# A feed-forward half in four sweeps of one batch each, with streamed weights and operands that are never stored

## The chip, the core and the metric

The kernel runs on one core of a Trainium2 chip. The metric is the device time of one execution in microseconds, the median of several runs. The engines are named as in the profile: PE (TensorE, matmul and transposes), PEld (its weight load), DVE (VectorE), ACT (ScalarE), POOL (GpSimd) and SP (SyncE, which here issues nearly all DMAs, in order, on one queue).

## What is computed

The input is 4 batches of 1024 rows with 2048 columns. An adaptive layer norm feeds a long convolution along the columns (the first half, not touched by the change), whose gated result is added to x. Then a second adaptive layer norm feeds a linear layer, to which a sum of 16 low-rank updates is added, and its gated result is added to x. Cut to this:

```python
h = _layernorm(x, axis=-1) * (1 + ca) + sa
x = x + ga * _L0_attn_ref(h, ...)
h = _layernorm(x, axis=-1) * (1 + cb) + sb
x = x + gb * _L0_ffn_ref(h, W, bias, A, Bf, coeffs, scales)
...
def _L0_ffn_ref(x, W, bias, A, Bf, coeffs, scales):
    out = jnp.einsum('bsd,od->bso', x, W) + bias
    xa = jnp.einsum('bsd,erd->ebsr', x, A)
    upd = jnp.einsum('ebsr,eor,e->bso', xa, Bf, coeffs * scales)
    return out + upd
```

ga and gb, sa and sb, ca and cb come from a small product of the conditioning vectors with a modulation matrix. In f32 the second linear layer is a product of 4096 x 2048 by 2048 x 2048.

## The kernel before

**First half.** A modulation product, the making of the convolution's Toeplitz matrices, then 32 row blocks (r = 0 to 31, 128 rows each) go through the convolution on PE. In gaps of it, the low-rank updates are merged into the weights and the weights are split and written to DRAM as `wcd` (function `merge`). Each row block's result is written to DRAM as `x1d`, with its mean and scale kept in `ln2` (`conv_post`).

**Feed-forward half.** The product is done by a scheme of seven products in place of eight: rows and columns of the left operand and of the weights are split in halves, seven sums of quarters of the left operand are each multiplied by a sum of quarters of the weights (number i, 0 to 6), and the four quarters of the output are sums of the seven products. Every f32 operand is held as two f16 numbers, a high and a low part; a product is high times high, high times low and low times high. So one 128x512 accumulator of one product takes 8 x 3 = 24 matmuls of 128x128 by 512 columns.

- `wcd` holds the seven weight sums for each of two column quarters q (512 columns in each half of the output's columns): 7 sums of 2 MiB for each q.
- Two passes, q = 0 and q = 1. In each, the seven weight sums of this q stay in SBUF (14 tiles of 1 MiB), and 16 units u of 256 rows go through (`ffn_unit`, L815 to L880).
- Pass q = 0 makes the left operands (`left`, L759 to L805): two row blocks of `x1d` are loaded (L765), normalized on ACT (L766), transposed on PE in groups of four (L776) and scaled from PSUM to SBUF on ACT (L778). Then four sums on DVE and seven casts on ACT (L788) and subtractions on DVE (L789) make the seven f16 pairs. Each pair is used and also written to DRAM (`lfd`, L790). This work is given out in small steps between the products of the units ahead (`tick`, with the plan `LPLAN`).
- Pass q = 1 loads those pairs again (`left_load`, L809).
- A unit's seven products run in the order 0, 4, 5, 1, 6, 2, 3. Three PSUM accumulators, X, Y and Z, take them; where two products are added to each other the second is accumulated on the first in PSUM (0 and 1 in X, 4 and 2 in Y, while Z takes 5, 6 and 3 as a running sum). ACT copies partial results out (L834), DVE adds them, multiplies with the gate (L849), adds the residual with the bias (L850), and SP stores the 128x512 block (L851). The residual's four blocks are loaded at the start of a unit (L843) and the bias is added to them at once (L844).
- The gate and bias rows of a batch are loaded as broadcasts twice per batch, and the gate is scaled on DVE (L1198).

**Order.** The code gives the instructions in one order, which is their priority; a scheduler at compile time puts each engine's instructions into a fixed order from it, by what it reckons to be ready. On the chip, each engine and each queue takes its list in order. PSUM has five accumulators of one bank for products (`ACC = 5`) and two for transposes (`TPS = 2`).

**Where the halves meet.** The first unit's operands are made in steps during the last two row blocks of the convolution (r = 30 and 31, `LEFT0`). Weights of the first product are loaded into tiles of their own when the merges are done (`early`), those of the second and third into the row tiles x0 to x3 of the first half as these come free.

Of the kernel before, what the change touches and what calls it, by code (L numbers as in the profile page):

```python
# [12 lines left out]
F32 = mybir.dt.float32  # L13
# [16 lines left out]
NU = 16  # L30
# [5 lines left out]
class Net:  # L36
# [722 lines left out]
    def left(self, pl, u, res):  # L759
        nc, v = self.nc, self.nc.vector  # L760
        b = u // 4
        xs = []
        for r in range(2):
            x = pl["x2"].tile([P, D], F32, tag=f"x2{r}", name="x2")
            nc.sync.dma_start(out=x, in_=self.x1d[2 * u + r])  # L765
            nc.scalar.activation(  # L766
                x, x, AF.Identity, bias=self.ln2[:, 2 * u + r, 0:1], scale=self.ln2[:, 2 * u + r, 1:2]
            )
            xs.append(x)
        yield  # L770
        t = pl["t"].tile([P, NC, 2, P], F32, tag="t", name="gt")
        for c0 in range(0, NC, 2):
            tp = self.tps.tile([P, 2, 2, P], F32, tag="t", name="tp2")
            for c in range(2):
                for r in range(2):
                    nc.tensor.transpose(tp[:, c, r], xs[r][:, ds(P * (c0 + c), P)], self.ident)  # L776
            for c in range(2):
                nc.scalar.activation(  # L778
                    t[:, c0 + c], tp[:, c], AF.Identity,
                    bias=self.sb[:, c0 + c, b : b + 1], scale=self.cb[:, c0 + c, b : b + 1],  # L780
                )
            yield
        a11, a12 = t[:, 0:HC, 0, :], t[:, HC:NC, 0, :]
        a21, a22 = t[:, 0:HC, 1, :], t[:, HC:NC, 1, :]

        def put(i, s):
            hl = pl["l"].tile([P, HC, 2, P], F16, tag="l", name="lf")
            nc.scalar.copy(hl[:, :, 0, :], s)  # L788
            v.tensor_tensor(hl[:, :, 1, :], s, hl[:, :, 0, :], SUB)  # L789
            STQ(nc).dma_start(out=self.lfd[u, i], in_=hl)  # L790
            res[i] = hl

        put(0, a11)
        s = pl["s"].tile([P, HC, P], F32, tag="s", name="s")
        v.tensor_tensor(s, a21, a22, ADD)
        put(4, s)
        v.tensor_tensor(s, s, a11, SUB)
        put(5, s)
        put(1, a12)
        v.tensor_tensor(a21, a11, a21, SUB)  # L800
        put(6, a21)
        v.tensor_tensor(s, a12, s, SUB)
        put(2, s)
        put(3, a22)
        yield  # L805

    def left_load(self, pl, u, i):
        hl = pl["l"].tile([P, HC, 2, P], F16, tag="l", name="lf")
        self.nc.sync.dma_start(out=hl, in_=self.lfd[u, i])  # L809
        return hl  # L810

    def left_again(self, pl, u):
        return {i: self.left_load(pl, u, i) for i in ORDER}

    def ffn_unit(self, pl, u, q, lf, wc, tick):  # L815
        nc, v = self.nc, self.nc.vector
        ps = {}

        def prod(i, name):
            first = name not in ps  # L820
            if first:
                ps[name] = self.acc.tile([P, 512], F32, tag="a", name="f" + name)
            n = 0
            for k in range(HC):
                for x, y in ((0, 0), (0, 1), (1, 0)):
                    nc.tensor.matmul(  # L826
                        ps[name], lf[i][:, k, x, :], wc[i][k // 4][:, k % 4, y, :],
                        start=(first and n == 0), stop=(n == 3 * HC - 1), skip_group_check=True,
                    )
                    n += 1  # L830

        def copy(name, tag):
            t = pl["e"].tile([P, 512], F32, tag=tag, name=tag)
            nc.scalar.copy(t, ps[name])  # L834
            return t

        def at(x, r, h):
            return x[ds(P * r, P), ds(1024 * h + 512 * q, 512)]

        xs = {}  # L840
        for r, h in ((0, 0), (1, 1), (0, 1), (1, 0)):
            x = pl["o"].tile([P, 512], F32, tag="o", name="xo")
            nc.sync.dma_start(out=x, in_=at(self.x1d[2 * u : 2 * u + 2].rearrange("r p d -> (r p) d"), r, h))  # L843
            v.tensor_tensor(x, x, self.gbias[:, h], ADD)  # L844
            xs[r, h] = x

        def finish(r, h, cv, t):
            x = xs[r, h]
            v.tensor_tensor(t, cv, self.gbt[:, h], MUL)  # L849
            v.tensor_tensor(x, x, t, ADD)  # L850
            STQ(nc).dma_start(out=at(self.io["out"][ds(256 * u, 256), :], r, h), in_=x)  # L851


        prod(0, "X")
        p1 = copy("X", "p1")
        tick()
        prod(4, "Y")
        p5 = copy("Y", "p5")
        tick()
        prod(5, "Z")  # L860
        p6 = copy("Z", "p6")
        tick()
        prod(1, "X")
        finish(0, 0, ps["X"], pl["e"].tile([P, 512], F32, tag="p7", name="fin"))
        v.tensor_tensor(p6, p6, p1, ADD)
        tick()
        prod(6, "Z")
        p7 = copy("Z", "p7")
        v.tensor_tensor(p5, p5, p1, ADD)
        v.tensor_tensor(p7, p7, p5, ADD)  # L870
        finish(1, 1, p7, p7)
        tick()
        prod(2, "Y")
        v.tensor_tensor(p6, p6, ps["Y"], ADD)
        finish(0, 1, p6, p6)
        tick()
        prod(3, "Z")
        v.tensor_tensor(p1, p1, ps["Z"], ADD)
        finish(1, 0, p1, p1)
        tick()  # L880


ORDER = (0, 4, 5, 1, 6, 2, 3)
# [7 lines left out]
LPLAN = ("LL", "LL", "LL", "LL", "L", "0", "")  # L891
# [4 lines left out]
EARLY = 2  # L896
RAW = 4
# [14 lines left out]
def net(ctx: ExitStack, tc: tile.TileContext, io):  # L912
# [7 lines left out]
    k.lfd = k.dram.tile([NU, 7, P, HC, 2, P], F16, tag="lfd", name="lfd")  # L920
# [156 lines left out]
    pr, wc, lf = {}, {}, {}  # L1077

    XW = {ORDER[1]: (0, 1), ORDER[2]: (2, 3)}

    def load_w(q, i):

        wc[i] = []
        for j in range(2):
            if i in XW:
                w = pl["x"].tile([P, D], F32, tag=f"x{XW[i][j]}", name=f"w{i}").bitcast(F16)
            else:
                w = pr["w" if i == ORDER[0] else "v"].tile([P, 2 * D], F16, tag=f"w{i}{j}", name=f"w{i}")
            wv = w.rearrange("p (k y n) -> p k y n", k=4, y=2)
            nc.sync.dma_start(out=wv, in_=k.wcd[q, i][:, 4 * j : 4 * j + 4])  # L1090
            wc[i].append(wv)

    def early():
        right.close()
        for name, bufs in (("w", 1), ("l", 8), ("t", 1), ("s", 1), ("x2", 1)):
            pr[name] = pool(p2, "p2" + name, bufs, "right")
        load_w(0, ORDER[0])

    def next_left(u):
        if u >= NU:  # L1100
            return iter(())
        lf[u] = {}
        return k.left(pr, u, lf[u])
# [3 lines left out]
    def step():  # L1107
        if r < R0:

            calls[0] += 1  # L1110
            if r > EARLY and calls[0] % 2 == 0:
                with tc.issue_after(k.lasta.ins), tc.issue_after(k.lastv.ins):
                    next(fill)
        elif "w" not in pr and next(fill, 0) == 0:
            early()
# [23 lines left out]
    for r in range(EARLY, 32):  # L1139
# [4 lines left out]
        if r == 31:  # L1144
            load_w(0, ORDER[1])
        if r == LEFT0:
            while "w" not in pr:
                step()
            lgen = next_left(0)
# [25 lines left out]
    take(lgen, 10)  # L1175
    gens = [next_left(1)]
    take(gens[0], 1)
    left.close()

    for name in ("v", "o", "e", "g"):  # L1180
        pr[name] = pool(p2l, "p2" + name, 5 if name == "o" else 1)
    for q in range(2):
        for i in ORDER:
            if i not in wc or q == 1:
                load_w(q, i)
            if q == 1:
                lf.setdefault(0, {})[i] = k.left_load(pr, 0, i)
        for u in range(NU):
            b = u // 4
            if u % 4 == 0:  # L1190
                ts_ = []
                for i in range(2):
                    t = pr["g"].tile([P, 2, 512], F32, tag=f"gb{i}", name=f"gb{i}")
                    src = k.gbd[i][b].rearrange("(h n) -> h n", h=2)[:, ds(512 * q, 512)]
                    nc.sync.dma_start(out=t, in_=src.partition_broadcast(P))
                    ts_.append(t)
                k.gbt, k.gbias = ts_
                nc.vector.tensor_scalar(k.gbt, k.gbt, k.ginv[:, b : b + 1], None, MUL)  # L1198
            plan = iter(LPLAN)

            def tick():
                if q == 1:
                    return
                for a in next(plan):
                    if a == "0":
                        gens[0] = next_left(u + 2)
# [64 lines left out]
```

## Time and profile before

| | us |
|---|---|
| runs: median of 3 (lowest to highest) | 2134.47 (2133.88 to 2139.61) |
| the profiled execution's own time | 2133.88 |
| its span, first to last instruction | 2132.1 |
| mean granted TensorE clock | 0.988 |
| first product of the feed-forward half starts | 911.2 |
| its second pass starts, about | 1553.5 |
| last product ends | 2126.7 |

| from 911 us on | DMAs, all on SP's queue |
|---|---|
| operands written to `lfd`, 512 KB each | 106 (112 in all) |
| operands read from `lfd`, 512 KB each | 112 |
| residual blocks read, 256 KB each | 128 |
| output blocks written, 256 KB each | 128 |
| rows of `x1d` read, 1 MiB each | 28 (32 in all) |
| weights read, 1 MiB each | 23 (28 in all) |
| gate and bias broadcasts, 512 KB each | 16 |

The span holds all that the engines do; the profiled time lies 1.8 us above it. In the tables of groups that follow, a line names the code line, the engine, the operation, what it writes and reads, the shapes, and how often; then busy time and the mean of one in ns, and the time for which the engine stood idle just before such instructions with what ended it. In a table of stretches, each row gives a stretch in us from the span's start, its length, each engine's busy time with the count of instructions, the granted clock as a fraction, the mean busy share of the 16 DMA engines and GB/s. A matmul's own duration (379 ns) is longer than the distance to the next one, since they are pipelined; the pace is read from the chain of waits, which merges a row of matmuls into one piece.

### The profile page before, as it was taken

To read this page: it belongs to the slowest core of one execution; us is meant where nothing else is said; L and a number is where in the kernel's file an instruction comes from. 1 tells how busy PE (TensorE), PEld (TensorE's weight loads), DVE (VectorE), ACT (ScalarE), POOL (GpSimd) and SP (SyncE) were. 2 spreads that over 40 slices of the span, in tenths; PEclk is the share of its full clock that TensorE was granted. 3 is DMA by queue.
4 is the path that set the end of the run, shared out by engine and by line. 5 is a ranking of instruction groups with operands and counts; after the bars stand their busy time and mean duration, and the time that the engine had idled before them with its cause. 6 is when DMAs were issued, how large, how long until landed. Compare 5 with 4: busy or idle time off the path is not lost.

```text
span 2132.1 us, 27801 instructions
## 1 busy us (share of the span) xinstructions
PE 2056.1 (96%) x10845; PEld 991.2 (46%) x10845; DVE 1271.3 (60%) x2226; ACT 888.0 (42%) x1564; POOL 22.8 (1%) x53
## 2 busy tenths in 40 slices
PE   6888999999999999999999999999999999999998
PEld 2333454444444455544555555555444444444444
DVE  5428798888879998755575565565533333332323
ACT  1324875666766776646555555555200000000000
POOL 1020000000000000000000000000000000000000
PEclk8899999999999999999999999999999999999999
DMA  9896868898887665487564564564794545454541
GB/s 404 322 345 255 327 237 316 338 337 305 342 314 291 226 243 202 172 342 261 210 229 173 216 226 170 217 228 167 294 346 160 186 148 181 165 167 158 178 154 69
DMA packets 131954, 512.97 MB, mean 241 GB/s; under 512 B 14432, under 2 KB 14960, under 8 KB 97262
## 3 DMA queue, kind: packets, MB, share of 16 engines
q1 hardware_dynamic: 130224, 506.92, 64.8%
q10 hardware_dynamic: 526, 2.63, 0.3%
q8 instruction: 85, 1.39, 0.3%
q0 software_dynamic: 1072, 1.65, 0.2%
q14 instruction: 47, 0.39, 0.0%
HBM read 355.55 MB, written 155.59 MB: 240 GB/s over the span
## 4 chain that ended last, share of the span: by engine, by line
PE 72%; DVE 10%; issue 7%; ACT 6%; DMA 5%; POOL 0%; SPq 0%; POOLq 0%; ACTq 0%; DVEq 0%
PE fZ L826 23%; PE fY L826 15%; PE fX L826 15%; PE ya L677 7%; PE yb L677 3%; PE tp L776 3%; PE modps L320 2%; PE lps L502 2%; ACT xt L642 1%; DVE wch L530 1%; DVE st L566 1%; DMA wm<-in_wmod 1%; DMA gsd<-rkg 1%; DMA x<-in_x 1%; DMA wcd<-wch 1%
## 5 line engine op out<-in xcount | busy, mean ns | idle before, releaser
L826 PEld LDWEIGHTS <-lf 128*128 128x128 f16 x5376 | 526.0, 98 | 620.8 <-issue 1.1
L826 PE MATMUL fZ<-w,lf 128*128 128x512 f16 x2304 | 514.1, 379 | 0.8 <-ACT p L834 0.8
L826 PE MATMUL fY<-w,lf 128*128 128x512 f16 x1536 | 342.1, 379 | 0.0
L826 PE MATMUL fX<-w,lf 128*128 128x512 f16 x1536 | 342.1, 379 | 0.0
L677 PEld LDWEIGHTS <-hc 128*128 128x128 f16 x2304 | 212.7, 98 | 219.4 <-issue 57.5
L677 PE MATMUL ya<-kh,hc 128*128 128x512 f16 (+3 forms) x768 | 203.8, 329 | 7.4 <-ACT qs L692 7.2
L844 DVE TENSOR_TENSOR xo<-xo,gb 128x512 f32<-128x512 f32 x128 | 87.6, 690 | 204.6 <-DMA xo<-x1d 191.7
L677 PE MATMUL yb<-kh,hc 128*128 128x512 f16 (+3 forms) x768 | 201.3, 327 | 2.5 <-DVE we L504 1.7
L677 PE MATMUL ya<-kh,hs 128*128 128x512 f16 (+3 forms) x768 | 189.9, 326 | 2.6 <-ACT hs L626 1.3
L834 ACT COPY p<-fZ 128x512 f32<-128x512 f32 x64 | 37.2, 582 | 292.3 <-PE fZ L826 276.3
L677 PEld LDWEIGHTS <-hs 128*128 128x128 f16 x1152 | 106.0, 98 | 111.4 <-issue 26.4
L778 ACT ACTIVATE gt<-tp,sb,cb 128x256 f32<-128x256 f32 x256 | 124.0, 570 | 66.7 <-PE tp L776 66.7
L834 ACT COPY p<-fX 128x512 f32<-128x512 f32 x32 | 18.7, 585 | 311.6 <-PE fX L826 241.7
L642 ACT ACTIVATE xt<-xt,cas 128x128 f32<-128x128 f32 x448 | 140.3, 393 | 9.8 <-DVE cas L588 9.1
L320 PE MATMUL modps<-wm,sct 128*32 128x512 f32 x768 | 116.1, 646 | 16.7 <-DMA wm<-in_wmod 16.7
L677 PE MATMUL ya<-kl,hc 128*128 128x512 f16 (+3 forms) x384 | 126.0, 328 | 0.0
L677 PE MATMUL yb<-kl,hc 128*128 128x512 f16 (+3 forms) x384 | 125.4, 327 | 0.0
L677 PE MATMUL ya<-kl,hs 128*128 128x512 f16 (+3 forms) x384 | 125.1, 326 | 0.0
L849 DVE TENSOR_TENSOR fin<-fX,gb 128x512 f32<-128x512 f32 x32 | 22.1, 692 | 128.2 <-PE fX L826 128.1
L566 DVE BATCH_NORM_STATS2 st<-x 128x6 f32<-128x512 f32 x128 | 81.6, 682 | 9.9 <-DMA x<-in_x 9.9
L502 PE MATMUL lps<-lbh,lac 128*128 128x512 f16 x256 | 86.3, 379 | 1.1 <-ACT lbh L476 1.1
L789 DVE TENSOR_TENSOR lf<-gt,lf 128x1024 f16<-128x1024 f32 x64 | 76.7, 1220 | 17.5 <-ACT lf L788 17.5
(289 smaller groups left out, 2124.4 us busy)
## 6 DMA issues: line engine op xcount, KB each, us to landing
wm<-in_wmod SPq DMA_DIRECT2D x96, 1024.0 KB
lfd<-lf SPq DMA_DIRECT2D x112, 512.0 KB
lf<-lfd SPq DMA_DIRECT2D x112, 512.0 KB
x<-in_x SPq DMA_DIRECT2D x32, 1024.0 KB
x1d<-y SPq DMA_DIRECT2D x32, 1024.0 KB
x<-x1d SPq DMA_DIRECT2D x32, 1024.0 KB
xo<-x1d SPq DMA_DIRECT2D x128, 256.0 KB
out<-xo SPq DMA_DIRECT2D x128, 256.0 KB
```

Source lines behind the costliest of these rows:

```text
L320: self.last = self.nc.tensor.matmul(self.modps[32 * g : 32 * g + 32, :], self.sct[:, j].rearrange("p r b -> p (r b)"), w[:, ds(512 * g, 512)],
L502: nc.tensor.matmul(ps, la[:, x, k, h], y[:, k, osl], start=(n == 0), stop=(n == 5))
L566: v.bn_stats(st[:, q], self.xs[r][:, ds(512 * q, 512)])
L642: nc.scalar.activation(xt[:, k], src, AF.Copy, scale=cas[:, k : k + 1])
L677: nc.tensor.matmul(pf[:, o:512], h, self.kf[f][z][:, ds(k0, 512 - o)], start=first, stop=(i == last and (x, z) == (1, 0)), skip_group_chec ...
L776: nc.tensor.transpose(tp[:, c, r], xs[r][:, ds(P * (c0 + c), P)], self.ident)
L778: nc.scalar.activation(t[:, c0 + c], tp[:, c], AF.Identity, bias=self.sb[:, c0 + c, b : b + 1], scale=self.cb[:, c0 + c, b : b + 1],)
L789: v.tensor_tensor(hl[:, :, 1, :], s, hl[:, :, 0, :], SUB)
L826: nc.tensor.matmul(ps[name], lf[i][:, k, x, :], wc[i][k // 4][:, k % 4, y, :], start=(first and n == 0), stop=(n == 3 * HC - 1), skip_grou ...
L834: nc.scalar.copy(t, ps[name])
L844: v.tensor_tensor(x, x, self.gbias[:, h], ADD)
L849: v.tensor_tensor(t, cv, self.gbt[:, h], MUL)
```

## The change

The feed-forward half is rewritten as a class `Ffn`.

- **Four sweeps** s = 0 to 3, one for each batch of 1024 rows, with two units u of 512 rows (the row halves of a unit are 256 rows, two row blocks rb). The loop over products is now outside: for each product i in the new order 0, 1, 5, 2, 6, 4, 3, all of q = 0, 1, u = 0, 1 and rb = 0, 1 are done, eight accumulators of 24 matmuls each.
- **Weights are streamed**: 4 sweeps x 7 products x 4 tiles of 1 MiB go through the four tiles x0 to x3; after the last accumulator of a q, the next two loads are issued (`load_w`).
- **Left operands** are kept as f32 quarters in SBUF (`quad`: six of the eight quads of a sweep in one pool, the other two and one buffer for a sum in another). Quads of 256 rows x 1024 columns are loaded (two loads of 512 KB, `xr`), normalized, transposed and scaled in six steps. For sweep 0 two quads are made ahead of the seam and six during the first two products; for later sweeps eight quads are made during the last four products of the sweep before, in the tiles that come free. The sums are made in place (`sum_steps`, five for each unit on 128x2048), and the f16 pairs of the next product in eight pieces of 512 columns from a ring of 12 (`piece_steps`). Nothing is written to DRAM; `lfd` is gone.
- **Products are no longer accumulated on each other in PSUM**: each of the eight accumulators of each product is taken out by itself (`outer`), with two running sums a and b in SBUF for each output place. Product 0 is copied to a by ACT; 5, 2 and 6 are one DVE add each; 1 and 3 finish one output block each and 4 finishes two.
- **Finishing**: the residual block (from a ring of six, fetched four ahead) gets its bias, the sum its gate, both are added and stored, all at the same place in the code (`finish`).
- **Gates** are loaded once per sweep as two 1 MiB broadcasts.

The core of the diff:

```diff
+    def load_w(self):
+        n = self.wn
+        if n >= len(self.wl):
+            return
+        self.wn += 1
+        i, t = self.wl[n]
+        w = self.wpool.tile([P, D], F32, tag=f"x{n % 4}", name="w").bitcast(F16)
+        w = w.rearrange("p (k y n) -> p k y n", k=4, y=2)
+        self.nc.sync.dma_start(out=w, in_=self.k.wcd[t // 2, i][:, ds(4 * (t % 2), 4)])
+        self.wt[n] = w
...
+    def quad_steps(self, s, u, hr, hc):
...
+        def load():
+            for rb in range(2):
+                x = self.pl["xr"].tile([P, D // 2], F32, tag="xr", name="xr")
+                nc.sync.dma_start(out=x, in_=k.x1d[8 * s + 4 * u + 2 * hr + rb][:, ds(1024 * hc, 1024)])
+                xs.append(x)
...
+    def piece_steps(self, i, u):
...
+        def piece(rb, kh):
+            src = self.q[LEFT[i] + str(u)][:, ds(4 * kh, 4), rb]
+            hl = self.pl["l"].tile([P, 4, 2, P], F16, tag="l", name="lf")
+            nc.scalar.copy(hl[:, :, 0, :], src)
+            nc.vector.tensor_tensor(hl[:, :, 1, :], src, hl[:, :, 0, :], SUB)
+            self.pieces[i, u, rb, kh] = hl
...
+    def side(self, s, m):
+
+        out = [[], [], [], []]
+        if (s, m) == (0, 0):
+            quads = [(0, (0, 0, 1)), (1, (1, 0, 1)), (2, (0, 1, 0)), (3, (0, 1, 1))]
+        elif (s, m) == (0, 1):
+            quads = [(0, (1, 1, 0)), (1, (1, 1, 1))]
+        elif m >= 3 and s + 1 < NB:
+            quads = [(2 * u, (u, *{3: (0, 1), 4: (0, 0), 5: (1, 0), 6: (1, 1)}[m])) for u in range(2)]
...
+    def finish(self, key, t):
+        v = self.nc.vector
+        n = self.fin.index(key)
+        x = self.xo.pop(n)
+        sl = ds(1024 * key[3] + 512 * key[4], 512)
+        v.tensor_tensor(x, x, self.gbias[:, sl], ADD)
+        v.tensor_tensor(t, t, self.gb[:, sl], MUL)
+        v.tensor_tensor(x, x, t, ADD)
+        out = self.k.io["out"].rearrange("(r p) d -> r p d", p=P)
+        STQ(self.nc).dma_start(out=self.at(out, *key), in_=x)
+        self.fetch(n + AHEAD)
+
+    def outer(self, i, u, rb, q, ps):
...
+        if i == 0:
+            nc.scalar.copy(a, ps)
+        elif i == 5:
+            v.tensor_tensor(b, a, ps, ADD)
+        elif i == 2:
+            v.tensor_tensor(a, b, ps, ADD)
+        elif i == 6:
+            v.tensor_tensor(b, b, ps, ADD)
+        else:
+            ts_ = []
+            for c, _ in FIN[i]:
+                t = temp()
+                v.tensor_tensor(t, b if c == "b" else a, ps, ADD)
+                ts_.append(t)
+            for t, (_, h) in zip(ts_, FIN[i]):
+                self.finish((u, rb, *h, q), t)
+
+    def plain(self, i, tick):
...
+        for q in range(2):
+            for u in range(2):
+                for rb in range(2):
+                    ps = self.k.acc.tile([P, 512], F32, tag="a", name="f")
+                    n = 0
+                    for kh in range(2):
+                        l, w = self.pieces[i, u, rb, kh], self.wt[self.w0 + 2 * q + kh]
+                        for c in range(4):
+                            for x, y in ((0, 0), (0, 1), (1, 0)):
+                                nc.tensor.matmul(
+                                    ps, l[:, c, x, :], w[:, c, y, :], start=(n == 0), stop=(n == 23), skip_group_check=True
+                                )
+                                n += 1
+                    if u and rb:
+                        self.load_w()
+                        self.load_w()
+                    self.outer(i, u, rb, q, ps)
+                    tick(2 * q + u, 1 - rb)
+        self.w0 += 4
...
+FIN = {1: (("a", (0, 0)),), 4: (("a", (0, 1)), ("b", (1, 1))), 3: (("b", (1, 0)),)}
+LEFT = {0: "00", 1: "01", 5: "s2", 2: "01", 6: "00", 4: "10", 3: "11"}
+AHEAD = 4
+ORDER = (0, 1, 5, 2, 6, 4, 3)
```

## The prediction

> **What bounds the kernel now.** I read the page first, then the stretches of the feed-forward half, then what TensorE waits for in it, then the end of the chain of waits. The page's first lines and one shape of each kind:
>
> ```profile
> span 2132.1 us, 27801 instructions
> ...
> PE 2056.1 (96%) x10845; PEld 991.2 (46%) x10845; DVE 1271.3 (60%) x2226; ACT 888.0 (42%) x1564; POOL 22.8 (1%) x53
> ...
> L826 PE MATMUL fZ<-w,lf 128*128 128x512 f16 x2304 | 514.1, 379 | 0.8 <-ACT p L834 0.8
> ```
>
> PE is busy 96% of the span, but a mean hides the stage that matters. The feed-forward half starts at 911.2 us and its last product ends at 2126.7. Its two passes as two stretches:
>
> ```profile
> core 0: us, PE busy (x) PEld busy (x) DVE busy (x) ACT busy (x) POOL busy (x), PEclk, DMA share, GB/s
> 911.20:1553.50 642.30, 640.68 (x3205) 320.08 (x3203) 372.17 (x452) 311.52 (x441) 0.00 (x0) 1.00 0.62 228
> 1553.50:2126.70 573.20, 573.16 (x2656) 259.62 (x2654) 185.51 (x274) 36.86 (x63) 0.00 (x0) 1.00 0.51 173
> ```
>
> PE is busy for 640.68 of 642.30 us and 573.16 of 573.20, at granted clock 1.00, with DVE, ACT and the DMA engines between 6% and 62%. All that PE waited for there is this:
>
> ```profile
> PE tp L776 <- ACT x L766: 0.8, 1, 0.8
> PE fZ L826 <- ACT p L834: 0.8, 1, 0.8
> ```
>
> Busy matmuls can still be slow ones, so I check their pace in the chain, and read the tail there too:
>
> ```profile
> 2116.30 5.18 PE fY L826 x24
> 2121.48 5.19 PE fZ L826 x24
> 2126.67 0.02 issue
> 2126.69 0.70 DVE p L878
> 2127.39 0.02 issue
> 2127.42 0.70 DVE p L849
> 2128.12 0.02 issue
> 2128.14 0.69 DVE xo L850
> ```
>
> 24 matmuls take 5.18 us, 215.8 ns for 512 columns, and the pace is the same in both passes. Eight transposes take 0.87 us (from the same chain), 109 ns each. So 5376 x 0.2158 + 480 x 0.109 = 1160.1 + 52.3 = 1212.4 us, and the measured busy sum is 1213.8. Nothing but PE's instruction count bounds this half, and the tail is three DVE steps and a store, 5.4 us.
>
> **The change on PE.** Before: 2 passes x 16 units x 7 products x 24 matmuls = 5376. After: 4 sweeps x 7 products x 8 accumulators (two column halves, two units, two row blocks) x 24 = 5376, of the same 128x128 by 512 f16 shape. Transposes: 16 units x 32 = 512 before; 32 quarter blocks (I say quads: 256 rows by 1024 columns) x 16 = 512 after. 32 of them stand ahead of 911.2 in both. Gain and loss on PE: 0.0 us. The change can therefore return only the 1.6 us of waits and can lose whatever makes PE wait. It works on bytes and on DVE, which have room; the rest is a search for new waits.
>
> **Removed.** 112 stores of operands and 112 loads, 512 KB each, 117.4 MB. No PE instruction waited for them. Of SP's queue they took long waits (operand stores behind DVE, loads behind the matmuls that free a buffer), none seen by PE: gain 0 on the path.
>
> **Added: weights streamed.** 112 loads of 1 MiB, 28 before: 88.1 MB more, so the whole moves 512.97 - 117.4 + 88.1 = 483.7 MB. The densest place is the sixth product (operand 4, two finished outputs per accumulator): 4.2 MB of weights, 4.2 of x, 4.2 of stores, 2.1 of rows for the next sweep = 14.7 MB. PE needs 8 x 5.18 + 32 x 0.109 = 44.9 us for it: 327 GB/s. What the queues can do, in two stretches of this trace:
>
> ```profile
> 911.00:921.00 10.00, 10.00 (x55) 5.17 (x54) 3.51 (x11) 4.71 (x8) 0.00 (x0) 1.00 0.97 371
> 921.00:931.00 10.00, 10.00 (x56) 5.55 (x55) 2.61 (x3) 5.78 (x11) 0.00 (x0) 1.00 1.01 427
> ```
>
> 427 GB/s with PE busy all 10 us: 14.7 MB are 34.4 us, 23% spare. The Trainium skill ("DMA: Bandwidth & Descriptors", section Specifications) speaks against the change here: it gives a core about 358 GB/s of HBM. By it the product would take 41.0 us, still inside 44.9 but with 9% spare, and the output rival below would gain weight; the trace's own 427 decides for me. A pair of weight loads, 2.1 MB, takes 4.9 us at 427. Its slots come free when the half product that read them ends; the next half product hides it, 4 x 5.18 = 20.7 us. If SP stands still for the longest wait that DVE had on x (7.8 us, DVE's list of waits) and landing costs what one x row pair shows beyond its bytes (7.72 us in the chain at 961.52 for two 1 MiB loads, so 7.7 - 4.9 = 2.8), it lands 7.8 + 4.9 + 2.8 = 15.5 us after release. Bound: 0 to, with that cover gone, 15.5 per change. I take 0.
>
> **Added: DVE sums instead of accumulation in PSUM.** Per sweep of 8 accumulators 3 products take one add, two take an add and three finishing steps (4), one takes 8, the first is copied by ACT: 8 x (3 + 8 + 8) = 152, or 608 in all, against 17 x 32 = 544 before. A 128x512 f32 step is 0.69 us; back to back I see starts 0.60 apart when independent (1234.43, 1235.03, 1235.63 on DVE) and 0.73 when each needs the one before (the tail above). So 365 to 444 us. The 40 sums on 128x2048 are not in this trace: twice the 1.22 of 128x1024 at most (2.45), and 1.22 + (1.22 - 0.69) x 2 = 2.28 by the slope; I take 2.3, 92 us. 224 piece subtractions by the 0.69 row of hs, 155 us. Four gate scalings of 2048 columns are 6 us (0.75 for 1024). DVE: at most 444 + 98 + 155 + 6 = 703 of 1216 us, 58% (before 558, 46%). ACT: 32 copies x 0.58 + 256 evictions x 0.57 + 224 piece copies x 0.62 + 64 norms of 1024 columns (between 0.58 and 2.09, nearest the 1.04 of 1024-column casts) x 1.04 = 370 us, 30%. Both lie under PE, except where bunched: the sixth product has 64 DVE steps and 8 piece subtractions, 43 us at 0.60 and 52 at 0.73, against 44.9 (41.4 in the last sweep). DVE starts after the first accumulator, so at worst it is done 5.2 + 52 - 44.9 = 12.3 us after PE's end of that product. Late next: the second unit's pieces, wanted 10.4 us (first row block, and by order earlier than the last 8 steps) and 15.5 us (second) after that end. Slack about 3 us in the worst pitch, 9 and more in the best. PSUM is no limit: five accumulators let PE run four tiles, 20.7 us, ahead. Price here: 0, bound 12.3 - 10.4 = 1.9 us x 4 sweeps.
>
> **Moved: row quads.** Each quad is two 512 KB loads into one pair of buffers, two norms on ACT, 16 transposes in four groups, 8 ACT evictions. The load waits for the transposes of the quad before it, and behind it on SP stand weight loads, x loads and stores. The order on the queues is not the code's: before, the x load of a unit leaves at 1017.58, just when the last transposes of the other end (1016.62 + 0.87), although in the code it stands two products later. So I expect it issued at release, about three tiles before its first transposes. Behind a weight pair: 4.9 + 2.5 + 2.8 + 2 x 1.04 = 12.3 us, against 15.5 from release or 10.4 from the two tiles that separate load and transposes in the code. Price 0 to 1.9 us each.
>
> **Gates and seam.** Once per sweep two 1 MiB gate loads wait for the last finishing step of the sweep before; queued behind them on SP are the first x loads, wanted a product (41 us) later: 0. At the seam the last convolution row loses 7 casts and 11 DVE steps of 1024 columns (13.4 us of DVE) and gets 8 pieces (5.5 us): no loss. Tail: add, multiply, add and a 256 KB store as now, 0; if the bias add stands last too, +0.73.
>
> **Sum.** The profiled execution took 2133.88 us, span 2132.1 and 1.8 around it, beside a median of 2134.47. 2133.88 - 1.6 (old waits) + waits of the new order. For these I take one wait of the size seen, 0.8, per sweep: 3.2. Together 2135.5 us; bounds of this case alone 2131 to 2140.
>
> **Rivals.** (1) Late rows: PE runs its list in order, so a group of transposes that stands ahead of its rows stops the matmuls behind. For: it is one of the two waits seen. Against: that was once in 28 loads, beside full queues. Place: 30 quads (all but the two ahead of the seam). Price 0.8 each as seen, 24 us, so 2133.9 - 1.6 + 24 = 2156; at 1.9 each 2189. It decides once rows land later than 10.4 us after a weight pair was issued and the order doesn't allow for it. (2) The output ring of the sixth product: six x buffers, a finish every 2.9 us, so a buffer must load, be used and be stored in 17.4 us. With 7.8 us of wait on x, DVE ends 12.3 + 7.8 = 20 us late, 4.6 beyond the 15.5, in four sweeps 18 us: 2150. SP behind it would bring the weights late too. For: 327 GB/s; against: 23% spare and the 0.60 pitch. (3) Faster: only PE's idle time ahead of the half can pay. From 700 to 911 PE is idle 10.1 us (94.0 and 95.9 busy of two 100 us stretches); if the change of buffers freed all, 2133.9 - 1.6 - 10.1 = 2122. Nothing there waits for what is removed.
>
> **How the numbers follow.** What can be told from no change is 0.3%, 6.4 us: 2128.1 to 2140.9. No change 0.61 (its own range 2131 to 2140), late rows 0.18, output ring 0.15, faster 0.06. Rivals (1) and (2) in their mild half end below 2153, so 2129 to 2153 leaves out about 0.2.
>
> **What would show it.** Right: 5376 product matmuls at 215.8 ns, PE idle under 6 us from the first to the last product, 484 MB, DVE near 57% of the half with its fullest stretch in each sixth product. Wrong: waits of transposes for ACT's norm of x (1), waits of products for pieces after each sixth product or for weights (2), another clock or pace than 1.00 and 215.8, or a half that starts later than 911.

## The result, and the profile after

The changed kernel takes 2172.6 us (median of four runs, 2169.2 to 2174.8) against 2134.7 us before. The ratio is 1.0171 with a 95% interval of 1.0151 to 1.0192: slower by 37.9 us by the medians, 36.5 by the ratio. The forecast was no change at 2135.5 us, with a range of 2129 to 2153. It was wrong.

The page of the profile after, with the two groups of PE that the change touches:

```profile
span 2170.8 us, 27852 instructions
PE 2075.2 (96%) x10845; PEld 990.9 (46%) x10845; DVE 1331.7 (61%) x2374; ACT 869.4 (40%) x1612; POOL 22.8 (1%) x53
DMA packets 113202, 483.61 MB, mean 223 GB/s; under 512 B 12576, under 2 KB 13104, under 8 KB 70830
L962 PE MATMUL f<-w,lf 128*128 128x512 f16 x5376 | 1181.5, 380 | 0.0
L806 PE MATMUL tp<-ident,xr 128*128 128x128 f32 x512 | 77.0, 279 | 23.1 <-ACT xr L799 21.4
```

The count of instructions on PE is the same, 10845, and so is the share that it is busy. The products wait for nothing (0.0). The transposes do: 23.1 us of idle time before them, nearly all until ACT's norm of the rows `xr`.

The whole feed-forward half as one stretch, from the first product to the end of the last (columns as in the stretches of before), and then the list of what PE waited for (us in total, times, longest), over all of it and again from 1010 us on, that is, without the first two products of the first sweep:

```profile
915.20:2165.20 1250.00, 1227.75 (x5859) 579.66 (x5856) 626.12 (x875) 333.31 (x549) 0.00 (x0) 0.99 0.51 178
```

```profile
PE tp L806 <- ACT xr L799: 20.5, 12, 3.6
...
PE tp L806 <- ACT xr L799: 16.9, 6, 3.6
```

The half takes 1250.0 us where it took 1215.5, so 34.5 of the loss are in it. Six waits make 16.9 us of that, 1.7 to 3.6 us each; they stand in pairs near 1186 and 1214, 1501 and 1528, 1815 and 1841. Counted in products (192 matmuls each), the first of each pair falls in the seventh accumulator of the sixth product of sweeps 0, 1 and 2, where the rows of the next sweep are made beside two finished blocks for each accumulator; the second falls in the third accumulator of the seventh product. (The expectations below put all six in the sixth.)

Four stretches behind these pauses, the same columns; the eighth is the granted clock (PEclk, after five engines' busy times):

```profile
1186.00:1193.00 7.00, 6.69 (x24) 3.40 (x25) 3.17 (x6) 2.46 (x6) 0.00 (x0) 0.59 0.63 200
1501.00:1506.00 5.00, 4.56 (x15) 1.99 (x16) 2.51 (x4) 1.91 (x4) 0.00 (x0) 0.66 0.66 217
1814.00:1820.00 6.00, 5.22 (x30) 3.10 (x31) 3.72 (x6) 4.08 (x9) 0.00 (x0) 1.00 0.65 191
1841.00:1846.00 5.00, 5.00 (x22) 2.69 (x23) 1.51 (x3) 1.02 (x2) 0.00 (x0) 0.74 0.16 56
```

PE is busy in them, but behind three of the six pauses at a lower clock: 0.41 x 7 + 0.34 x 5 + 0.26 x 5 = 5.9 us lost while the profile counts PE as busy. That is why the list of waits alone does not hold the loss.

Now one of the pauses. First PE's own row of instructions in order of time (start, length of the row, line, what), then SP's in the same time (start, time from the first issue to the end of the last, line, transfer, how many):

```profile
1163.03 1.04 PE L806 MATMUL tp<-ident,xr 128*128 128x128 f32 x8
1163.90 0.81 PE L962 MATMUL f<-w,lf 128*128 128x512 f16 x3
1164.74 0.66 PE L806 MATMUL tp<-ident,xr 128*128 128x128 f32 x4
1165.23 15.06 PE L962 MATMUL f<-w,lf 128*128 128x512 f16 x69
1180.13 0.27 PE L806 MATMUL tp<-ident,xr 128*128 128x128 f32 x1
1180.24 2.54 PE L962 MATMUL f<-w,lf 128*128 128x512 f16 x11
1186.31 0.90 PE L806 MATMUL tp<-ident,xr 128*128 128x128 f32 x3 [3.54 <-ACT xr L799]
```

```profile
1165.37 0.32 SPq L793 DMA_DIRECT2D xr<-x1d  x1
1166.35 0.99 SPq L923 DMA_DIRECT2D out<-xo  x2
1167.43 2.86 SPq L777 DMA_DIRECT2D w<-wcd  x2
1173.09 0.94 SPq L923 DMA_DIRECT2D out<-xo  x2
1174.12 5.24 SPq L910 DMA_DIRECT2D xo<-x1d  x3
1179.41 0.42 SPq L793 DMA_DIRECT2D xr<-x1d  x1
```

The last transposes of a quad end at 1165.2 and free both of its row buffers. The first row load of the next quad leaves at once, at 1165.37. In SP's list nine entries stand between it and the second: two pairs of stores, two weight loads and three fetches of x. It leaves at 1179.41, 14 us after its buffer was free. What SP waited for between the two (us in total, times, longest):

```profile
SPq L923 <- DVE xo L921: 3.8, 4, 2.8
SPq L910 <- DMA out<-xo: 2.7, 1, 2.7
SPq L777 <- PE f L962: 2.1, 1, 2.1
```

Stores wait for DVE to finish their blocks, a fetch waits for a slot of the ring of six, that is, for an earlier store to land, and weights wait for their tile: together 8.6 of the 14 us. At all six places the second load left 12.7 to 14.2 us after its buffer was free. Between 1194.6 and 1207.1, ahead of the wait in the seventh product, SP waited 4.7 us for DVE's blocks and 2.2 for a weight tile, and not for the ring. PE's list has the first transpose of the first row block at 1180.13 (one instruction, it runs) and after eleven more products those of the second, whose rows land and are normed only at 1186.3.

The short pauses can be read in the same lines: three products that take 0.65 us stand between 1163.90 and 1164.74, 0.84 us. I read this as the last group of four transposes waiting 0.19 us for one of two PSUM banks that ACT must empty (tested below with three banks). There are 24 such pauses of 0.19 or 0.27 us beside later quads, 5.5 us in all.

### The profile page after: what moved, and what is told of

Read it like the earlier page. It is cut to its first block, busy times and chain, and to the rows that moved or that the text cites. A ratio compares the mean times of both kernels' runs of the same rounds, so it can differ in the third digit from the quotient of the medians.

```text
span 2170.8 us, 27852 instructions
## 1 busy us (share of the span) xinstructions
PE 2075.2 (96%) x10845; PEld 990.9 (46%) x10845; DVE 1331.7 (61%) x2374; ACT 869.4 (40%) x1612; POOL 22.8 (1%) x53
## 2 busy tenths in 40 slices
DMA packets 113202, 483.61 MB, mean 223 GB/s; under 512 B 12576, under 2 KB 13104, under 8 KB 70830
## 4 chain that ended last, share of the span: by engine, by line
PE 67%; DVE 12%; DMA 7%; issue 7%; ACT 6%; SPq 0%; POOL 0%; POOLq 0%; ACTq 0%; DVEq 0%
PE f L962 48%; PE ya L676 7%; PE yb L676 4%; PE tp L806 2%; DMA xr<-x1d 2%; PE modps L319 2%; PE lps L501 2%; DVE st L565 1%; DMA x<-in_x 1%; DMA out<-xo 1%; DVE wch L529 1%; ACT xt L641 1%; DMA gsd<-rkg 1%; ACT xr L799 1%; DVE hc L626 1%
## 5 line engine op out<-in xcount | busy, mean ns | idle before, releaser
L962 PE MATMUL f<-w,lf 128*128 128x512 f16 x5376 | 1181.5, 380 | 0.0
L799 ACT ACTIVATE xr<-xr,ln 128x1024 f32<-128x1024 f32 x64 | 79.3, 1240 | 149.0 <-DMA xr<-x1d 148.8
L806 PE MATMUL tp<-ident,xr 128*128 128x128 f32 x512 | 77.0, 279 | 23.1 <-ACT xr L799 21.4
L921 DVE TENSOR_TENSOR xo<-xo,e 128x512 f32<-128x512 f32 x128 | 85.1, 685 | 1.3
L920 DVE TENSOR_TENSOR e<-e,gb 128x512 f32<-128x512 f32 x128 | 85.0, 684 | 0.8
L806 PEld LDWEIGHTS tp<-ident,xr 128*128 128x128 f32 x512 | 58.8, 141 | 55.4 <-ACT xr L799 28.6
L626 DVE TENSOR_TENSOR hc<-xt,hc 128x1024 f16<-128x1024 f32 x64 | 77.6, 1218 | 10.4 <-ACT hc L625 10.3
L938 DVE TENSOR_TENSOR ca<-cb,f 128x512 f32<-128x512 f32 x32 | 22.0, 687 | 94.2 <-PE f L962 94.2
```

The lines of the kernel that those rows point to most:

```text
L626: v.tensor_tensor(pair[1][:, sl], src, pair[0][:, sl], SUB)
L799: nc.scalar.activation(x, x, AF.Identity, bias=k.ln2[:, r, 0:1], scale=k.ln2[:, r, 1:2])
L806: nc.tensor.transpose(tp[:, c, rb], xs[rb][:, ds(P * (c0 + c), P)], k.ident)
L920: v.tensor_tensor(t, t, self.gb[:, sl], MUL)
L962: nc.tensor.matmul(ps, l[:, c, x, :], w[:, c, y, :], start=(n == 0), stop=(n == 23), skip_group_check=True)
```

## The experiments

All times below are medians; each ratio is to the kernel before on the same chip and in the same hours. "Half" is the time from the start of the first product to the end of the last in the profiled execution: 1215.5 before, 1250.0 after. The start of the first product scattered between 908.9 and 913.3 us in six experiments that leave the first half alone (911.2 before, 915.2 after). So the 4.0 us by which the changed kernel's half starts later are probably scatter in the main; no run shows it.

**Rows issued by POOL.**

```diff
-                nc.sync.dma_start(out=x, in_=k.x1d[8 * s + 4 * u + 2 * hr + rb][:, ds(1024 * hc, 1024)])
+                nc.gpsimd.dma_start(out=x, in_=k.x1d[8 * s + 4 * u + 2 * hr + rb][:, ds(1024 * hc, 1024)])
```

> One edit: the row loads of the quads (xr) are issued by POOL instead of SP; same bytes, same buffers. Theory A (order on SP): in the sixth product the second row load of a quad stands on SP behind x fetches that wait for a slot of the ring of six, so PE stands 17.9 us before transposes in three sweeps and then runs some 13.7 us at half clock (6.8 us lost). The six waits go: about 2148 us (2144 to 2153), no half clock in the half. Theory B (bytes: the DMA engines are full there): rows land as late as before, 2168 to 2175. Rival C (descriptors made by POOL are slower than the wait they save): new waits of ACT's norm for xr, 2172 or more.

Measured: 2163.5 us, ratio 1.0127 (1.0106 to 1.0149), half 1244.7. From 1010 us on, the list of PE's waits is empty: all six waits and the low clock behind them are gone, with the same bytes in the same places. So the bytes (theory B) are not the cause: the DMA engines are busy 0.77 of the sixth and of the seventh product of sweep 0, against 0.72 and 0.75 in the changed kernel. The total missed the 2148 I expected, since before 1010 us, in the opening of sweep 0, the waits for the norm rose from 3.6 to 17.4 us. The longest of them, first PE's row in this run, then the same place in the changed kernel:

```profile
926.39 4.70 PE L962 MATMUL f<-w,lf 128*128 128x512 f16 x21
938.53 0.69 PE L806 MATMUL tp<-ident,xr 128*128 128x128 f32 x2 [7.44 <-ACT xr L799]
```

```profile
928.24 9.01 PE L962 MATMUL f<-w,lf 128*128 128x512 f16 x41
937.09 0.38 PE L806 MATMUL tp<-ident,xr 128*128 128x128 f32 x2
```

Two stretches of this run there, columns as before:

```profile
927.00:935.00 8.00, 4.09 (x19) 1.67 (x17) 6.39 (x10) 2.73 (x6) 1.43 (x2) 1.00 0.97 320
935.00:945.00 10.00, 6.47 (x26) 3.85 (x27) 0.69 (x1) 4.97 (x8) 0.00 (x0) 0.66 0.07 30
```

POOL issued these rows at 926.98, 0.6 us after their buffer was free, so they did not leave late. They took 10.3 us to land beside full DMA engines (0.97), where the 64 row loads of this run took 5.9 in the median, and PE's list has the transposes after 21 products where the changed kernel has 41. Once they had landed the DMA engines had little to do (0.07), and again the clock fell (0.66). Rival C, slower descriptors, is not shown by this: the new waits come with another order in PE's list.

**No rows in the sixth product.**

```diff
-        elif m >= 3 and s + 1 < NB:
-            quads = [(2 * u, (u, *{3: (0, 1), 4: (0, 0), 5: (1, 0), 6: (1, 1)}[m])) for u in range(2)]
+        elif m in (3, 4) and s + 1 < NB:
+            quads = [(2 * u, (u, *{3: (0, 1), 4: (0, 0)}[m])) for u in range(2)]
+        elif m == 6 and s + 1 < NB:
+            quads = [(2 * u + h, (u, 1, h)) for u in range(2) for h in range(2)]
...
-            if first:
+            if first or m == 6:
                 out[z] += st
```

> The two quads made during the sixth product of sweeps 0 to 2 move to the seventh, which now makes four, one for each unit and column half. Theory A: the waits belong to the sixth product, where two finished blocks for each accumulator fill SP's list; they go, about 2148 us (2144 to 2155). As predicted in rival 1 (each quad costs by itself): the waits move with the rows to the seventh product, 2168 to 2178. Theory B (bytes): gain too, since the seventh product moves fewer bytes; this run does not tell A from B, e1 does.

Measured: 2175.6 us, ratio 1.0199 (1.0170 to 1.0228), half 1253.3. The list of PE's waits from 1010 us on:

```profile
PE tp L806 <- ACT xr L799: 21.2, 10, 5.2
```

The waits moved with the rows: all ten stand in the seventh product. My expectation that they belong to the sixth product as a place fell (three of the six had never stood there). The edit does more than move two quads: it also puts all six steps of a quad into one stretch, so four quads in one product, each loading only when the one before it is transposed, wait as well. I take from it that the time between the issue of a row load and the transposes that read it decides, not the product.

**Transposes spread two and two.**

```diff
-                out[z] += st[:3]
-                out[z + 1] += st[3:]
+                out[z] += st[:4]
+                out[z + 1] += st[4:]
```

> The four transpose groups of a later quad stand two and two in its two stretches instead of one and three. The profile shows 24 pauses of 0.19 and 0.27 us beside these groups, 5.5 us in all. If they are the wait for one of two PSUM slots that ACT empties: half or more goes, 2167 to 2170. If they are a price of changing between transposes and products: unchanged, 2172 to 2174. The first group still waits in the sixth product, with a second behind it, so the 17.9 us stay.

Measured: 2139.1 us, ratio 1.0027 (1.0017 to 1.0037), half 1220.7. I had expected only the short pauses to go. They went, all 24, as waits for PSUM banks would (e4 changes the banks themselves); but the six long waits went as well, which I had not foreseen. SP's row in the same product of the same sweep shows why, and the stretch there shows the effect:

```profile
1159.22 1.69 SPq L793 DMA_DIRECT2D xr<-x1d  x2
1161.54 0.94 SPq L923 DMA_DIRECT2D out<-xo  x2
1162.53 2.26 SPq L777 DMA_DIRECT2D w<-wcd  x2
```

```profile
1180.00:1190.00 10.00, 10.00 (x52) 5.04 (x51) 8.94 (x16) 4.87 (x9) 0.00 (x0) 1.00 0.83 270
```

With the transposes elsewhere in the order, the list that the compiler makes for SP has both row loads side by side here, ahead of stores and weights. At the six places the second load left 0.5 to 4.2 us after its buffer was free, where the changed kernel had 12.7 to 14.2. The next experiment takes the second load away and leaves the transposes at their places in the code.

**Both row blocks in one load.**

```diff
-            for rb in range(2):
-                x = self.pl["xr"].tile([P, D // 2], F32, tag="xr", name="xr")
-                nc.sync.dma_start(out=x, in_=k.x1d[8 * s + 4 * u + 2 * hr + rb][:, ds(1024 * hc, 1024)])
-                xs.append(x)
+            x = self.pl["xr"].tile([P, 2, D // 2], F32, tag="xr", name="xr")
+            r = 8 * s + 4 * u + 2 * hr
+            nc.sync.dma_start(out=x, in_=k.x1d[r : r + 2][:, :, ds(1024 * hc, 1024)].rearrange("r p d -> p r d"))
+            xs.extend((x[:, 0], x[:, 1]))
...
-        for name, bufs in (("q", 1), ("xr", 2), ("l", LR)):
+        for name, bufs in (("q", 1), ("xr", 1), ("l", LR)):
```

> The two row loads of a quad (512 KB each) become one of 1 MiB into one buffer of both row blocks; the transposes keep their places in the code (one group, then three). In SP's list of the changed kernel the second row load of a quad of the sixth product stands ten places behind the first, behind two weight loads, four stores and three x fetches; here there is no second one. Theory A (order on SP): the six waits of the sixth product go, with the half clock behind them, 17.9 + 6.8 us: 2148 us (2144 to 2153); the short pauses by PSUM slots stay. If the spread of e3 helped only since its transposes stand elsewhere in PE's list: unchanged, 2168 to 2175.

Measured: 2143.1 us, ratio 1.0048 (1.0030 to 1.0066), half 1227.2. The groups of transposes stand in the code as in the changed kernel, one and then three, and the 24 short pauses are all there. The six long waits are not. SP and PE at the same place:

```profile
1160.53 0.37 SPq L793 DMA_DIRECT2D xr<-x1d  x1
1161.40 0.94 SPq L923 DMA_DIRECT2D out<-xo  x2
1162.43 2.90 SPq L777 DMA_DIRECT2D w<-wcd  x2
```

```profile
1160.29 15.06 PE L962 MATMUL f<-w,lf 128*128 128x512 f16 x69
1175.18 0.60 PE L806 MATMUL tp<-ident,xr 128*128 128x128 f32 x4
1175.62 5.34 PE L962 MATMUL f<-w,lf 128*128 128x512 f16 x24
```

69 products run, then four transposes, without a pause, where the changed kernel had 69, one transpose, eleven products and 3.5 us of waiting. The half is 1250.0 - 1227.2 = 22.8 us shorter, and the six waits and the lost clock read from the profile after are 16.9 + 5.9 = 22.8. That they agree to a tenth is luck, since the waits of the opening rose from 3.6 to 5.2 us in this run; and 2143.1 lies under the 2144 to 2153 I expected. At the six places the one load left 0.2 to 3.1 us after its buffer was free. Theory A holds: it was the place of the second row load in SP's list.

**Three transpose banks.**

```diff
-ACC, TPS = 5, 2
+ACC, TPS = 4, 3
```

> Three PSUM banks for transposes and four for products instead of two and five, in the whole kernel. If the short pauses are slots: they go, minus 5.5, about 2167. If four accumulators are too few for DVE's lag in the sixth product: products wait for DVE there, plus 2 us and more for each sweep, 2175 to 2190. The convolution and the merges, which use the same five, may lose by themselves: read by the start of the first product, 915.2 us now.

Measured: 2153.8 us, ratio 1.0090 (1.0075 to 1.0105), half 1244.5. The short pauses of the later sweeps are gone, as expected of slots, and no product waits for DVE: four accumulators are enough. The long waits after 1010 us are three instead of six, 15.2 us together, since this too moves the lists: before each of the three the second row load left 16.4 or 16.5 us after its buffer was free, and at the other three places both loads left within 2.2 us. The total fell by more than the half's 5.5 and below the 2167 I expected: the first product starts at 901.7 us, 13.5 earlier, though only the count of banks changed ahead of it.

**The kernel before with three transpose banks**, the same line changed there, as a control.

> The kernel before with three transpose banks and four accumulators, as a control for e4, where the first product started at 901.7 us against 909.3 to 915.4 in the others. If that gain belongs to the first half, which both kernels share: first product near 902, 2124 to 2130. If it is scatter of the first half: 2131 to 2138. Four accumulators may make products of the second half wait: then over 2138.

Measured: 2131.0 us, ratio 0.9989 (0.9978 to 1.0000), first product at 906.3, half 1215.1. A gain of 0.1% (0.2% at most by its interval), so most of e4's early start was scatter or does not carry over.

**Spread and three banks; spread and one load.** Both as the diffs above together.

> e3 and e4 together. The sixth product's waits are gone by e3, the short pauses by either; left are the waits of the first sweep (5.2 us in e3). First half as in e4: 2139 - 7 = 2132 (2128 to 2136). If e4's single late group in each sixth product comes back: 2143 and more.

Measured: 2136.1 us, ratio 1.0012 (1.0000 to 1.0025), half 1221.0. The 2132 I expected did not come: the half is that of the spread alone (1220.7), and the first product starts at 909.0, not at e4's 901.7.

> e3 and e5 together. Theory A: each alone frees the sixth product, so both together give nothing more there: 2139 (2135 to 2142). The first sweep's quads, of which each waits for the buffers of the one before, may gain or lose 2 us by loading both blocks at once.

Measured: 2138.7 us, ratio 1.0019 (1.0003 to 1.0035), half 1219.3. As expected, two cures of the same place don't add up. What is left in both are 4 to 6 us of waits in the opening of sweep 0, before 1010 us.

**Two row buffers in the opening**, on top of spread and one load.

```diff
-            x = self.pl["xr"].tile([P, 2, D // 2], F32, tag="xr", name="xr")
+            tag = "s2" if alt else "xr"
+            x = self.pl["q2" if alt else "xr"].tile([P, 2, D // 2], F32, tag=tag, name="xr")
...
-            st = self.quad_steps(s if first else s + 1, u, hr, hc)
+            st = self.quad_steps(s if first else s + 1, u, hr, hc, (s, m) == (0, 0) and z % 2 == 1)
```

> e8, and in the opening (first product of sweep 0) every second quad loads its rows into the buffer of the sum s2, which is not used yet. Theory A2: the waits left in e8, 4.2 us in four groups between 945 and 985 us, are a load that can only start when the transposes before it have ended, since there is one row buffer; two of the three places get a second buffer. The waits go below 2 us, first to last product 1219.3 - 2.5 = 1217 us, time about 2136 (2132 to 2139). If the rows are late by order or by bytes beside the weights of the opening instead: waits as before, 1219 us.

Measured: 2136.0 us, ratio 1.0003 (0.9988 to 1.0018), half 1216.5. The waits fell from 4.2 to 1.9 us, as expected: one row buffer was the cause of that part. Of the 1.9, 1.2 are waits for ACT to empty a transpose bank.

**The same with three transpose banks.**

> e9 with three transpose banks and four accumulators. If e6's small gain in the first half holds here: first product 3 us earlier than in e9's kind, 2133 (2129 to 2137), level with the kernel before within 0.1%. It can't be clearly faster than before: PE's count alone gives 5376 x 0.2158 + 480 x 0.109 = 1212.4 us from first to last product, 3 us under the 1215.5 of before.

Measured: 2129.8 us, ratio 0.9976 (0.9964 to 0.9988), half 1215.6. This is faster than the kernel before by 0.24% and than the changed one by 43 us. I had written that it can't be clearly faster than before, and it is, by 0.12 to 0.36%. Its half in the profiled execution is that of before (1215.6 against 1215.5), so the gain hardly lies in the four sweeps. The control e6 (2131.0) speaks for the three banks in the first half; the profiled execution of e10 was the slowest of its twelve (2133.4), so its trace does not show where the gain lies.

## Why the prediction was wrong, point by point

- **PE's count and pace: right.** 5376 products and 512 transposes, at 215.8 ns and 109 ns where nothing waits. The bound of 1212.4 us lies 3 us under the half of before (1215.5) and of the best repaired kernel (1215.6).
- **Bytes: right in sum, not in place.** 483.61 MB against 483.7 worked out. The weights were never late: no product waited for a load. The sixth product was to move 327 GB/s; the first one moved 247 (262 in e5) and the seventh 260 (272), so it was not clearly the densest place. That the DMA engines suffice there was shown by e1 and e5.
- **DVE and ACT: right.** DVE was busy 626 us of the half, under the bound of 703; the sums over 2048 columns took 2.28 to 2.29 us against 2.3. No product waited for pieces or accumulators. Two details were off: 626 us are 50% of the half, not the 57% named as a sign, and DVE was fullest in the seventh product (38.8 of 47.8 us in sweep 0), not the sixth (37.7 of 51.9). The norm of 1024 columns took 1.24 us, not 1.04; ACT had room for it.
- **Moved row quads: this step failed.** I wrote that a row load would be "issued at release", from one row of the trace before, and priced it at 0 to 1.9 us for each quad. It held for the first of a quad's two loads and not for the second, which left 12.7 to 14.2 us after release at the six places in the sixth and seventh products. That took 16.9 us of waits and 5.9 of lost clock, where the sum had 0 for the quads and 3.2 for all new waits. I had counted the x fetches, stores and weights on SP and set them down as standing behind the row load; the compiled list had them between the two loads, and whatever waits in front, a store for DVE, a fetch for a store or a weight load for its tile, holds everything behind it.
- **Rival 1 named the mechanism** (transposes ahead of their rows stop PE) and gave it 0.18; its wait, of transposes for ACT's norm, is the one that came. Its place and size were off: not 30 quads at 0.8 us but six at 1.7 to 3.6, and 3.6 us in the opening. Rival 2 named the output ring of the sixth product, but took it to reach PE through DVE's lag. The ring's wait had a part, in SP's list ahead of a row load: 2.7 us of the 14 in the pause shown, and none before the wait of the seventh product.
- **Two terms were missing.** Three of the four pauses of over 3 us cost the clock as well, 5.9 us here, and groups of three transposes outrun two PSUM banks, 5.5 us. I had copied the cost of the old groups of two.
- **The sum**: 16.9 (six waits) + 5.9 (clock) + 5.5 (banks) + 3.6 (opening) - 1.6 (old waits) = 30.3 of the 34.5 us in the half. Of the rest, some 4 us, 2 belong to the same waits: the list counts each from a matmul's own end, 379 ns after its start, while the next could have started after 216. The other 2 stand in distances between transposes, under a tenth of a microsecond each; I have not tied them to a cause.

Why the compiler's list puts the second load so far down in the one order and beside the first in the other is not shown: no run tested it, only its effect.

## What to carry to other kernels

Where an engine is full, moving work that it doesn't do can still cost, through the order of the issue queue: for every load that feeds the full engine, ask what stands before it in that queue and what the front of that queue waits for, not only when its buffer is free. Loads that are needed together were safer here as one transfer. A rule drawn from one instance of an order (a load that left at release) says nothing about the same load in another list.

## What the hardware showed that I had not expected

Pauses of PE of 3.6, 3.5 and 3.2 us were followed by a lower clock, one of 3.1 us and those under 2 us were not (rows 1186, 1501, 1841 against 1814 above). The price behind a pause was 1.3 to 2.9 us, up to four fifths of the pause itself.

The length of a pause alone does not decide. In e4 one of 1.9 us was followed by a lower clock, in e2 one of 3.5 us was not (PE's row with the pause, then the stretch behind it):

```profile
975.33 2.04 PE L806 MATMUL tp<-ident,xr 128*128 128x128 f32 x9 [1.91 <-ACT xr L799]
975.50:979.00 3.50, 3.50 (x14) 2.34 (x14) 1.78 (x3) 2.84 (x6) 0.00 (x0) 0.51 0.48 150
```

```profile
1840.87 0.44 PE L806 MATMUL tp<-ident,xr 128*128 128x128 f32 x2 [3.51 <-ACT xr L799]
1840.80:1844.30 3.50, 2.79 (x15) 1.46 (x16) 0.22 (x2) 1.26 (x2) 0.00 (x0) 1.00 0.63 222
```

In the traces' records of the granted clock, the low stretches (0.50) begin on a grid of 3.41 us that runs through the whole execution, and in the half they last one or two steps of it: in the changed kernel from 1184.86 (two steps), 1502.30 and 1840.22 (one each). In the halves of all twelve runs there are 12 such falls. In the step ahead of each PE stood idle for 0.64 of the step or more, and in every other step at full clock for 0.62 or less (idle counted from 216 ns after the start of a matmul, 109 after that of a transpose). The 1.9 us of e4 lay within one step; the 3.5 us of e2 fell on two, 0.58 of the one and 0.52 of the other. The Trainium skill ("TensorE: Matmul & The Clock Gate", Part 1) says that the array falls to half clock after an idle window of about 3.4 us and that these windows run freely; the traces agree on the windows and differ on the idle, since a window idle for about two thirds was enough.
